# v after q and k, gelus of fc1 behind the next chunk's products, and two PSUM tiles let go one by one, in a two-layer kernel that a planner orders

## Chip, cores and metric

One core of a Trainium2 chip runs the whole kernel. Five engines work beside each other, each through its own queue in order: TensorE (PE, with PEld for its weight loads), VectorE (DVE), ScalarE (ACT), GpSimd (POOL) and SyncE (SP, which issues DMAs). The metric is the device time of one execution in microseconds (us); a kernel's time is the median of its runs.

## The reference

Two layers on x of shape (8, 192, 64, 64) in float32. Layer 0 is window attention that keeps 16 keys per query, and an MLP; layer 1 is a Fourier mixer with a tiny pointwise MLP on (real, imaginary), and an MLP. Cut to what matters:

```python
# layer 0, tokens of one image; windows of 8 x 8 tokens, 6 heads of 32
shortcut = layer_norm(xs)
q, k, v  = split(windows(shortcut) @ qkv_w.T + qkv_b)
attn = einsum(l2n(q), l2n(k)) * temperature
attn = where(attn >= 16th largest of the row, attn, -100) ; attn = softmax(attn + rpb)
x2  = shortcut + (attn @ v) @ proj_w.T + proj_b
x2  = x2 + gelu(layer_norm(x2) @ fc1_w.T + fc1_b) @ fc2_w.T + fc2_b
# layer 1
f   = fft2(layer_norm(x))                       # per channel, 64 x 64
h   = gelu([f.real, f.imag] @ fc1_w.T + fc1_b) @ fc2_w.T + fc2_b
x   = x + real(ifft2(h))
out = x + gelu(layer_norm(x) @ mlp1_w.T + mlp1_b) @ mlp2_w.T + mlp2_b
```

Gelu is the exact one; the Fourier transforms are matrix products.

## The kernel before

An image is cut into 8 bands of 512 tokens; the 192 channels are kept as 128 + 64, and the last 64 channels of two half bands are laid on 128 partitions, so that a product over 192 channels is one product on 128 rows of the array and two on 64 rows that run side by side. For each band of layer 0 there are `front` (transpose, normalization, products of q, k and v, norms of q and k), `attention` twice (half bands `hb`: scale q and k, transposes `qt`, scores `s`, top 16 on DVE, softmax, `at`, product with v `po`) and `back` (projection `pp`, then `mlp`). Layer 1 goes by groups of 16 channels: `forward` (products `fa` along rows of the transform and `fz` along the other axis), `pointwise` twice (products `fh`, gelu on ACT, products `fo`), `inverse` (`fb`, `fy`); and by bands: `leave` (`mlp`, transposes `pz`, store).

All these are Python generators. Each `yield op(engine, weight, mode, get, put, after, done)` offers one block of instructions to the planner `issue` (line 33), which keeps a clock for each engine in its own units, knows for each offered block when its inputs and its buffers are there, and always picks one of those that can begin first, with urgency by due time. The order in which blocks are picked is the order of instructions in each engine's queue. A generator offers its next block only when the last has been picked, so the order of `yield`s within a generator is a fixed order within that band's work, while different bands, layers and images are interleaved freely. `get` and `put` count buffers: `ps` are the PSUM tiles, of which there are four of two banks each, `h` the gelu outputs, `xa` scratch, and so on. `mode` names how the array is divided; the planner charges 20 units where it changes on PE and 130 units where ACT changes between exp and gelu. A block with `EITHER` goes to ACT or DVE, whichever the planner sees finish first; the scaling of q and k goes to POOL or DVE, the square to ACT or POOL.

The places that the change touches:

- `mlp` (from line 551): three chunks of fc1, `fp` = 0, 1, 2, each with a product on 128 rows (`part_a`, L587) and on 64 rows (`part_b`, L600); chunk 1 has them in the other order, so that the sequence of chunk 0, 1, 2 is 128, 64, 64, 128, 128, 64. After each chunk `gelu` (L571, two ACT instructions) is offered, which frees the chunk's PSUM tile. After all three, `mo` (L630) needs all three gelus.
- `front` (from line 643): for p = 0 and 1 (halves of the tokens) products of q and k into `pq` (L744 on 128 rows, L758 on 64, L761 the bias) and of v into `pv` (L745 and L758) are in the same blocks, and `pv` stays open over both. The first block asks for two PSUM tiles at once. `squares` copies `pq` out (L786), squares (L708 on ACT or L710 on POOL), sums (L712); after p = 1 `norms` raises to the power -1/2 on POOL for each half band (L730); `values` copies `pv` out.
- `forward` (from line 981): two PSUM tiles `fz` are copied into one SBUF tile (L1032) by two DVE instructions in one block, then a row is corrected (L1037).

Copies that can go to either engine are all recorded at L786.

Of the kernel before, what the change touches and what calls it, by code (L numbers as in the profile page):

```python
# [15 lines left out]
C = 192  # L16
# [3 lines left out]
BAND = 512  # L20
# [8 lines left out]
def op(engine, weight, mode=None, get="", put="", after=None, done=None, put_too=""):  # L29
    return engine, weight, mode, get.split(), (put + " " + put_too).split(), after, done  # L30
# [108 lines left out]
def kernel(  # L139
# [18 lines left out]
    nc = tc.nc  # L158
# [9 lines left out]
    def psum(name):  # L168
        return psp.tile([128, 2, 512], FP, tag="ps", name=name)
# [4 lines left out]
        ps=4, xt=XT_BUFS, xn=1, qk=1, vv=2, att=ATT_BUFS, qkt=1, sm=2, ot=1, hn=2, xa=2,  # L174
# [69 lines left out]
    wqkv = load_ab("wqkv", 3 * C)  # L244
# [29 lines left out]
    qb3 = ctile("qb3", [128, 2 * C], BF)  # L274
    ones3 = ctile("ones3", [128, 128], BF)
# [275 lines left out]
    def mlp(src, nm, w1, fc1_bias, w2, then=None):  # L551

        mv = yield from statistics(src, nm)
        yield op("pool", 0, get="xa")
        to, pair = tokens("xa", 2, f"xa_{nm}")
        last = yield from normalized(to, pair, src, mv, nm)
        if then is not None:
            yield then()
        yield op("pe", 66, "full", get="ps hn", put="xa", after=last)
        pc = flat(f"lc_{nm}")  # L560
        to_channels(pc, pair, to)
        done = yield op(EITHER, (80, 96), put="ps")
        hn = strip("hn", 2, f"hn_{nm}")
        copy(done, hn, pc[:, :ROW])
        hs = []

        def gelu(fp, ph):
            yield op("act", 138, "gelu", put="ps", done=("gelu", nm, fp))
            h = sb.tile([128, 2, BAND], FP, tag="h", name=f"h_{nm}_{fp}", bufs=H_BUFS)
            for k in range(2):  # L570
                nc.scalar.activation(  # L571
                    h[:, k].rearrange("p (t n) -> p t n", t=2),
                    ph[:, :, k * HALF : (k + 1) * HALF],
                    AF.Gelu,
                    bias=fc1_bias[:, 2 * fp + k : 2 * fp + k + 1],
                )
            hs.append(h)

        for fp in range(3):


            fs = [slice((2 * fp + k) * 128, (2 * fp + k + 1) * 128) for k in range(2)]

            def part_a(first):
                for k, f in enumerate(fs):
                    for t in range(2):
                        nc.tensor.matmul(  # L587
                            ph[:, t, k * HALF : (k + 1) * HALF],
                            w1[0][:, f],
                            hn[:, t * HALF : (t + 1) * HALF],  # L590
                            start=(first and k == 0),
                            stop=not first,
                            skip_group_check=True,
                        )

            def part_b(first):
                for k, f in enumerate(fs):
                    for t in range(2):
                        rows = slice(64 * t, 64 * t + 64)
                        nc.tensor.matmul(  # L600
                            ph[:, t, k * HALF : (k + 1) * HALF],
                            w1[1][rows, f],
                            hn[rows, BAND:ROW],
                            start=(first and k == 0),
                            stop=not first,
                            skip_group_check=True,
                        )
# [12 lines left out]
        last = [("gelu", nm, fp) for fp in range(3)]  # L620
        for half in range(2):
            if half == 0:
                yield op("pe", 384, "full", get="ps", after=last)
                acc = psum(f"mo_{nm}")
            else:
                last = yield op("pe", 384, "full", put="h h h")
            for f in range(3 * half, 3 * half + 3):
                for t, j in PAIRS:
                    q = 2 * t + j
                    nc.tensor.matmul(  # L630
                        acc[:, j, t * C : (t + 1) * C],
                        hs[f // 2][:, f % 2, q * 128 : (q + 1) * 128],
                        w2[:, f, ORDER[t]],
                        start=(f == 0 and t == 0),
                        stop=(f == 5),
                        skip_group_check=True,
                    )
        return acc, last
# [4 lines left out]
    def front(b, i):  # L643

        nm = f"{b}_{i}"
# [14 lines left out]
        done = yield op(EITHER, (80, 96), put="ps")  # L660
# [5 lines left out]
        last = yield from normalized(xt, pair, pair, mv, f"a{nm}")  # L666
# [7 lines left out]
        for t, j in PAIRS:  # L674
            q = 2 * t + j
            for h in range(2):
# [17 lines left out]
        places = ("qk", "h") if more else ("qk", "vv")  # L694
# [40 lines left out]
        def values(whole):  # L735
            done = yield op(EITHER, (80, 96), put="ps", after=[whole], done=("vv", b, i))
            copy(done, vv.rearrange("p t a c -> p t (a c)"), pv[:, :, : 2 * C])

        for p in range(2):
            def part_a(first):  # L740
                for t in range(2):
                    tok = xn[:, (2 * t + p) * 128 : (2 * t + p + 1) * 128]
                    flags = dict(start=first, stop=not first, skip_group_check=True)
                    nc.tensor.matmul(pq[:, t, : 2 * C], tok, wqkv[0][:, : 2 * C], **flags)  # L744
                    nc.tensor.matmul(  # L745
                        pv[:, t, p * C : (p + 1) * C], tok, wqkv[0][:, 2 * C :], **flags
                    )

            def part_b(first):
                flags = dict(skip_group_check=True, stop=not first)  # L750
                for to, cols in (
                    (pq[:, :, : 2 * C], slice(0, 2 * C)),
                    (pv[:, :, p * C : (p + 1) * C], slice(2 * C, 3 * C)),
                ):
                    for t in range(2):
                        rows = slice(64 * t, 64 * t + 64)
                        tok = xn[rows, BAND + p * 128 : BAND + (p + 1) * 128]
                        nc.tensor.matmul(to[:, t], tok, wqkv[1][rows, cols], start=first, **flags)  # L758
                for t in range(2):
                    rows = slice(64 * t, 64 * t + 64)  # L760
                    nc.tensor.matmul(  # L761
                        pq[:, t, : 2 * C], ones3[rows], qb3[rows], start=False, **flags
                    )
# [217 lines left out]
    def forward(b, n):  # L981

        nm = f"{b}_{n}"
# [12 lines left out]
        for q in range(4):  # L996
# [4 lines left out]
                start=True,  # L1001
                stop=True,
# [303 lines left out]
```

## Time and profile before

| what | value |
|---|---|
| median of 3 runs (lowest, highest) | 4932.9 us (4930.42, 4936.1) |
| the profiled execution's own time | 4943.11 us |
| its span, first to last instruction | 4941.3 us |
| mean granted TensorE clock | 0.977 |
| instructions in the span | 147,257 |
| largest groups on ACT: L1050 gelu of fh | 815.1 us busy, x768, mean 1112 ns |
| on POOL: L730 power of the norms | 551.9 us busy, x128, mean 4311 ns |
| on PE: L630 mo_b and mo_d | 518.0 and 512.3 us busy, x3072 each, mean 327 ns |
| ACT table loads before exp (L858), fh (L1050), h (L571) | x110, x64, x47, 1283 ns each |

In a line of a group, out<-in are the program's names, then come shapes, the count, busy time, the mean of one, and the engine's idle time before it with what ended most of it. A float32 matmul leaves two records. A wait's line has the engine and instruction that waited, after the arrow the one whose end released it, then the sum, the number of times and the longest, all in us. In a line of windows come the stretch, its length, then busy time and count of PE, PEld, DVE, ACT and POOL, the granted clock, the DMA share and GB/s.

### The profile page before, as it was taken

The numbers are of one execution on the slowest core, as the hardware profiler recorded it, in microseconds if no ns is written. First come the engines' busy times: TensorE is split into PE (matmuls) and PEld (weight loads), VectorE is DVE, ScalarE is ACT, GpSimd is POOL, SyncE is SP. The second block draws the span as 40 slices with busy tenths as digits, with TensorE's granted clock in tenths as the row PEclk, the third lists the DMA queues.
The fourth block names the chain that finished last, engine by engine and source line by source line (L and its number), as shares of the span: only waits on it lengthen the run. The fifth ranks groups of instructions, "written<-read, shape, count | busy, mean of one in ns | idle before, by whom it ended". The sixth has DMA issues, their size and how long they took to land.

```text
span 4941.3 us, 147257 instructions
## 1 busy us (share of the span) xinstructions
PE 4702.8 (95%) x63818; PEld 3780.0 (76%) x63818; DVE 2797.7 (57%) x10326; ACT 2744.7 (56%) x3866; POOL 2381.0 (48%) x2208
## 2 busy tenths in 40 slices
PE   6888999999999999999999999999999999999989
PEld 4667777886778877888678877788777887778768
DVE  6778566456665466655665556645666546562112
ACT  3555666446655566555755566645666456653553
POOL 5677555346554455454653555545555445541100
PEclk7898999999999999999999999999999999999999
DMA  2000000000000000000000000000000000000000
GB/s 55 11 8 11 9 9 5 23 14 9 9 12 17 18 6 9 13 19 15 9 5 14 22 14 6 9 14 24 9 6 9 20 18 9 2 2 20 9 2 26
DMA packets 54112, 64.09 MB, mean 13 GB/s; under 512 B 17583, under 2 KB 36218, under 8 KB 53466
## 3 DMA queue, kind: packets, MB, share of 16 engines
q1 hardware_dynamic: 53454, 54.68, 3.8%
q8 instruction: 502, 8.22, 0.7%
q14 instruction: 144, 1.18, 0.1%
q10 hardware_dynamic: 12, 0.00, 0.0%
HBM read 29.29 MB, written 25.17 MB: 11 GB/s over the span
## 4 chain that ended last, share of the span: by engine, by line
PE 85%; ACT 5%; DVE 5%; POOL 3%; issue 2%; DMA 0%; SPq 0%; ACTq 0%; DVEq 0%; POOLq 0%
PE mo_d L630 10%; PE mo_b L630 9%; PE fh L1067 8%; PE mh_d L587 7%; PE fo L1094 7%; PE mh_b L587 7%; PE mh_d L600 4%; PE mh_b L600 4%; PE pq L744 3%; ACT fh L1050 3%; PE qt L804 2%; PE fa L997 2%; PE at L871 2%; PE fb L1115 2%; PE fy L1142 2%
## 5 line engine op out<-in xcount | busy, mean ns | idle before, releaser
L1050 ACT ACTIVATE fh<-fh,ab 128x1024 f32<-128x1024 f32 x768 | 815.1, 1112 | 163.9 <-PE fh L1067 160.2
L854 POOL TENSOR_TENSOR s<-s,top 128x768 f32<-128x768 f32 x128 | 193.8, 1514 | 917.5 <-DVE s L851 870.8
L730 POOL TENSOR_TENSOR nrm<-nrm,mhalf 128x24 f32<-128x24 f32 x128 | 551.9, 4311 | 10.7
L630 PE MATMUL mo_b<-wfc,h_b 128*128 128x192 f32 x3072 | 518.0, 327 | 0.0
L630 PE MATMUL mo_d<-wmlp,h_d 128*128 128x192 f32 x3072 | 512.3, 327 | 0.0
L630 PEld LDWEIGHTS mo_b<-wfc,h_b 128*128 128x128 f32 x3072 | 499.2, 190 | 10.3 <-issue 5.8
L630 PEld LDWEIGHTS mo_d<-wmlp,h_d 128*128 128x128 f32 x3072 | 498.6, 190 | 7.2 <-issue 4.6
L1067 PE MATMUL fh<-fz,w1p 32*128 32x248 f32 (+1 forms) x6144 | 467.6, 404 | 30.1 <-ACT fh L1050 23.3
L571 ACT ACTIVATE h_d<-mh_d,fcb 128x512 f32<-128x512 f32 x384 | 242.1, 684 | 436.0 <-PE mh_d L600 278.1
L1067 PEld LDWEIGHTS fh<-fz,w1p 32*128 32x128 f32 x6144 | 293.0, 185 | 149.5 <-issue 67.3
L844 DVE MAX8 top<-s 128x8 f32<-128x64 f32 x1536 | 320.9, 209 | 129.0 <-ACT s L786 127.9
L1094 PE MATMUL fo<-fh,w2p 128*32 128x264 f32 (+1 forms) x6144 | 387.2, 389 | 3.9 <-ACT fh L1050 2.3
L846 DVE MAX8 top<-s 128x8 f32<-128x64 f32 x1536 | 349.9, 228 | 53.4
L587 PE MATMUL mh_b<-hn_b,wfc_a 128*128 128x256 f32 x1536 | 377.0, 389 | 3.2 <-ACT hn_b L786 1.9
L587 PE MATMUL mh_d<-hn_d,wmlp_a 128*128 128x256 f32 x1536 | 370.7, 386 | 0.8 <-ACT hn_d L786 0.8
L864 POOL TENSOR_TENSOR s<-s,rsum 128x768 f32<-128x768 f32 x128 | 191.2, 1494 | 300.4 <-DVE top L844 144.5
L587 PEld LDWEIGHTS mh_b<-hn_b,wfc_a 128*128 128x128 f32 x1536 | 280.0, 191 | 67.7 <-issue 26.5
L587 PEld LDWEIGHTS mh_d<-hn_d,wmlp_a 128*128 128x128 f32 x1536 | 280.6, 190 | 55.3 <-issue 18.1
L845 DVE MATCH_REPLACE8 s<-top,s 128x64 f32<-128x64 f32 x1536 | 320.3, 209 | 0.1
L1094 PEld LDWEIGHTS fo<-fh,w2p 128*32 128x32 f32 x6144 | 185.6, 111 | 152.8 <-issue 33.4
L571 ACT ACTIVATE h_b<-mh_b,fcb 128x512 f32<-128x512 f32 x384 | 243.1, 686 | 97.3 <-PE mh_b L600 50.6
L1180 DVE TENSOR_TENSOR zt<-mo_d,xy 128x768 f32<-128x768 f32 x64 | 61.3, 957 | 377.2 <-PE mo_d L630 345.5
(220 smaller groups left out, 9311.2 us busy)
## 6 DMA issues: line engine op xcount, KB each, us to landing
xin<-in_x SPq DMA_DIRECT2D x64, 256.0 KB
out<-z SPq DMA_DIRECT2D x64, 256.0 KB
xin<-in_x SPq DMA_DIRECT2D x128, 64.0 KB
out<-z SPq DMA_DIRECT2D x128, 64.0 KB
wfc<-in_wfc SPq DMA_DIRECT2D x1, 576.0 KB
wmlp<-in_wmlp SPq DMA_DIRECT2D x1, 576.0 KB
wfc_a<-in_wfc SPq DMA_DIRECT2D x1, 384.0 KB
wfc_b<-in_wfc SPq DMA_DIRECT2D x2, 192.0 KB
```

Of the source, the lines that this page charges most:

```text
L571: nc.scalar.activation(h[:, k].rearrange("p (t n) -> p t n", t=2), ph[:, :, k * HALF : (k + 1) * HALF], AF.Gelu, bias=fc1_bias[:, 2 * fp + ...
L587: nc.tensor.matmul(ph[:, t, k * HALF : (k + 1) * HALF], w1[0][:, f], hn[:, t * HALF : (t + 1) * HALF], start=(first and k == 0), stop=not ...
L600: nc.tensor.matmul(ph[:, t, k * HALF : (k + 1) * HALF], w1[1][rows, f], hn[rows, BAND:ROW], start=(first and k == 0), stop=not first, skip ...
L630: nc.tensor.matmul(acc[:, j, t * C : (t + 1) * C], hs[f // 2][:, f % 2, q * 128 : (q + 1) * 128], w2[:, f, ORDER[t]], start=(f == 0 and t ...
L730: nc.gpsimd.tensor_tensor(nf, nf, mhalf[:, :24], ALU.pow)
L844: nc.vector.max(first, of)
L845: nc.vector.match_replace(s2, first, of, -3.0e38)
L846: nc.vector.max(top[:, k // 4, k % 4, 8:16], s2)
L854: nc.gpsimd.tensor_tensor(s, s, top[:, :, :, 0:1].to_broadcast(shape), ALU.subtract)
L1050: nc.scalar.activation(hs[hf, k], ph, AF.Gelu, bias=ab[:, 0:1])
L1067: nc.tensor.matmul(phs[k // 2][:, k % 2, cols], w1p[i][rows, hf].rearrange("p h v -> p (h v)"), fz[rows, :] if rhs is None else zu[rows, : ...
L1094: nc.tensor.matmul(po[rows, :] if i == 0 else pou[rows, :, 1 : U - 1], w2p[i][:, hf].rearrange("p a v -> p (a v)"), hs[hf, k // 2][:, k % ...
```

## The change

Three edits, and with them the order that the planner makes of everything.

1. In `front` the products of q and k for p = 0 and p = 1 come first, in blocks of their own (`qk_a`, `qk_b`), each with its `squares` offered behind it; the products of v for both p follow in two blocks, 128 rows and then 64 rows, into a `pv` that is asked for only then. The first block asks for one PSUM tile in place of two.
2. In `mlp` the gelu of chunk `fp - 1` is offered after the products of chunk `fp`; the last gelu follows after the loop. Since a gelu no longer follows directly on its products, it names them in `after`.
3. In `forward` the two copies out of `fz` are two blocks, each of which lets one PSUM tile go; the correction of the row goes with the second.

Matmuls, copies, and their sizes are the same; the number of ACT table loads and the engine of a copy, scale or square follow from the planner.

```diff
-        def gelu(fp, ph):
-            yield op("act", 138, "gelu", put="ps", done=("gelu", nm, fp))
+        def gelu(fp, ph, last):
+            yield op("act", 138, "gelu", put="ps", after=[last], done=("gelu", nm, fp))
...
-                yield op(
+                last = yield op(
                     "pe", weight, kind, get=get, put="hn" if fp == 2 and n == 1 else "", after=after
                 )
...
-            yield from gelu(fp, ph)
+            if fp > 0:
+                yield from gelu(fp - 1, *held_)
+            held_ = ph, last
+        yield from gelu(2, *held_)
         last = [("gelu", nm, fp) for fp in range(3)]
...
+        def qk_a(pq, p, first):
+            for t in range(2):
+                tok = xn[:, (2 * t + p) * 128 : (2 * t + p + 1) * 128]
+                nc.tensor.matmul(
+                    pq[:, t, : 2 * C],
+                    tok,
+                    wqkv[0][:, : 2 * C],
...
+        def qk_b(pq, p, first):
...
+        yield op("pe", 128, "full", get=f"ps {places[0]} {places[1]}", after=[normal, "qkv"])
+        pq = psum(f"pq_{nm}_0")
+        qk_a(pq, 0, True)
+        last = yield op("pe", 80, "row64")
+        qk_b(pq, 0, False)
+        yield squares(0, pq)
+        yield op("pe", 80, "row64", get="ps", after=[])
+        pq = psum(f"pq_{nm}_1")
+        qk_b(pq, 1, True)
+        yield op("pe", 128, "full")
+        qk_a(pq, 1, False)
+        yield squares(1, pq)
+        yield op("pe", 128, "full", get="ps", after=[])
+        pv = psum(f"pv_{nm}")
         for p in range(2):
-            def part_a(first):
...
-            if p == 0:
-                yield op("pe", 192, "full", get=f"ps ps {places[0]} {places[1]}", after=[normal, "qkv"])
-                pq, pv = psum(f"pq_{nm}_{p}"), psum(f"pv_{nm}")
-                part_a(True)
-                yield op("pe", 112, "row64")
-                part_b(False)
-            else:
-                yield op("pe", 112, "row64", get="ps", after=[])
-                pq = psum(f"pq_{nm}_{p}")
-                part_b(True)
-                whole = yield op("pe", 192, "full", put="xn")
-                part_a(False)
-            yield squares(p, pq)
+            for t in range(2):
+                nc.tensor.matmul(
+                    pv[:, t, p * C : (p + 1) * C],
+                    xn[:, (2 * t + p) * 128 : (2 * t + p + 1) * 128],
+                    wqkv[0][:, 2 * C :],
...
+        whole = yield op("pe", 64, "row64", put="xn")
+        for p in range(2):
...
         yield values(whole)
...
-        yield op("dve", 118, put="ps ps", done=("fz", b, n))
         fz = sb.tile([128, 16 * U], FP, tag="fz", name=f"fz_{nm}", bufs=2)
         for k in range(2):
+            yield op("dve", 43 + 33 * k, put="ps", done=("fz", b, n) if k else None)
             nc.vector.tensor_copy(
```

More of the change, by code (lines that the diff above doesn't have):

```diff
@@ L737, in values @@
             copy(done, vv.rearrange("p t a c -> p t (a c)"), pv[:, :, : 2 * C])
-        for p in range(2):
-            def part_a(first):
[L741 to L763, printed above, removed]
-            if p == 0:
-                yield op("pe", 192, "full", get=f"ps ps {places[0]} {places[1]}", after=[normal, "qkv"])
-                pq, pv = psum(f"pq_{nm}_{p}"), psum(f"pv_{nm}")
-                part_a(True)
-                yield op("pe", 112, "row64")
-                part_b(False)
-            else:
-                yield op("pe", 112, "row64", get="ps", after=[])
-                pq = psum(f"pq_{nm}_{p}")
-                part_b(True)
-                whole = yield op("pe", 192, "full", put="xn")
-                part_a(False)
-            yield squares(p, pq)
@@ new lines, in qk_a @@
+        def qk_a(pq, p, first):
[5 more added lines that the diff above has]
+                    wqkv[0][:, : 2 * C],
+                    start=first,
+                    stop=not first,
+                    skip_group_check=True,
+                )
+        def qk_b(pq, p, first):
+            flags = dict(skip_group_check=True, stop=not first)
+            for t in range(2):
+                rows = slice(64 * t, 64 * t + 64)
+                tok = xn[rows, BAND + p * 128 : BAND + (p + 1) * 128]
+                nc.tensor.matmul(
+                    pq[:, t, : 2 * C], tok, wqkv[1][rows, : 2 * C], start=first, **flags
+                )
+            for t in range(2):
+                rows = slice(64 * t, 64 * t + 64)
+                nc.tensor.matmul(pq[:, t, : 2 * C], ones3[rows], qb3[rows], start=False, **flags)
@@ new lines, in front @@
+        pv = psum(f"pv_{nm}")
+        for p in range(2):
+            for t in range(2):
+                nc.tensor.matmul(
+                    pv[:, t, p * C : (p + 1) * C],
+                    xn[:, (2 * t + p) * 128 : (2 * t + p + 1) * 128],
+                    wqkv[0][:, 2 * C :],
+                    start=(p == 0),
+                    stop=False,
+                    skip_group_check=True,
+                )
+        whole = yield op("pe", 64, "row64", put="xn")
+        for p in range(2):
+            for t in range(2):
+                rows = slice(64 * t, 64 * t + 64)
+                nc.tensor.matmul(
+                    pv[:, t, p * C : (p + 1) * C],
+                    xn[rows, BAND + p * 128 : BAND + (p + 1) * 128],
+                    wqkv[1][rows, 2 * C :],
+                    start=False,
+                    stop=True,
+                    skip_group_check=True,
+                )
```

## The prediction

> **What bounds the kernel now.** I read the engine totals and the 40 slices first, then the windows, PE's waits in the opening and in the long middle, and last single stretches of the timeline. Engine totals and the chain's shares from the page:
>
> ```profile
> PE 4702.8 (95%) x63818; PEld 3780.0 (76%) x63818; DVE 2797.7 (57%) x10326; ACT 2744.7 (56%) x3866; POOL 2381.0 (48%) x2208
> ...
> PE   6888999999999999999999999999999999999989
> PEclk7898999999999999999999999999999999999999
> ...
> PE 85%; ACT 5%; DVE 5%; POOL 3%; issue 2%; DMA 0%; SPq 0%; ACTq 0%; DVEq 0%; POOLq 0%
> ```
>
> PE is busy for 95% of the span and is 85% of the chain; no other engine passes 57%. Only the first four slices (500 us) leave PE clearly idle, and there the granted clock is below full as well. Three windows size this (first number after the stretch is PE's busy time):
>
> ```profile
> 0.00:625.00 625.00, 524.17 (x6540) 420.97 (x6540) 452.70 (x1774) 317.02 (x488) 409.64 (x356) 0.89 0.07 19
> 625.00:4700.00 4075.00, 3958.34 (x54711) 3181.09 (x54710) 2303.91 (x8432) 2323.90 (x3230) 1951.67 (x1816) 0.99 0.04 12
> 4700.00:4941.30 241.30, 220.26 (x2572) 177.99 (x2568) 41.14 (x121) 103.81 (x149) 19.68 (x36) 0.98 0.05 14
> ```
>
> PE idles 100.8 us in the opening, 116.7 in the middle, 21.0 at the end: 238.5 together. The change can save only there, or in how tightly the busy part runs. What PE waits for, opening first, then middle (total us, times, longest):
>
> ```profile
> PE qt L804 <- DVE qk L798: 27.4, 4, 12.1
> PE qt L804 <- POOL qk L798: 21.2, 3, 14.0
> PE s L821 <- ACT qkt L786: 14.2, 12, 2.4
> PE at L871 <- POOL s L864: 12.0, 7, 5.3
> ```
>
> ```profile
> PE fh L1067 <- ACT fh L1050: 23.3, 26, 1.6
> PE fz L1022 <- ACT fh L1050: 15.3, 16, 1.9
> PE lc L539 <- ACT fh L1050: 10.2, 16, 1.0
> ...
> PE lt L653 <- ACT fh L1050: 9.0, 6, 1.5
> PE qt L804 <- ACT fh L1050: 8.1, 19, 0.5
> ```
>
> Half of the opening's idle time, 48.6 us in seven waits, is qt (the transposes that begin attention of a band) waiting for scaled q and k, which is the end of `front`'s chain: product, copy, square, sum, norms on POOL, scale. In the middle the names differ but the releaser is one: ACT's gelu of fh. lt and lc do not read fh, so what they wait for is the PSUM tile that this gelu empties; these five lines are 65.9 of 116.7 us.
>
> The busy part hides a second loss. Timeline of PE near the end (start, us, instruction):
>
> ```profile
> 4854.10 1.13 PE L600 MATMUL mh_d<-hn_d,wmlp_b 64*128 64x256 f32 x8
> 4855.16 8.07 PE L630 MATMUL mo_d<-wmlp,h_d 128*128 128x192 f32 x48
> ...
> 4866.82 2.00 PE L600 MATMUL mh_d<-hn_d,wmlp_b 64*128 64x256 f32 x16
> 4868.74 1.99 PE L587 MATMUL mh_d<-hn_d,wmlp_a 128*128 128x256 f32 x8
> ```
>
> From start to start, eight L600 records (products on 64 rows) take 1.06 us where a product on 128 rows follows, and a run of sixteen takes 1.92, so the first eight, which their own kind follows, take 0.86. A change of tile size costs some 0.1 to 0.2 us. Over all 1,242 gap-free changes between 625 and 4700 us, the same subtraction (start to start, less the median of the same group followed by its own kind) gives a mean of 0.107 us.
>
> [...] the opening has waits of 12 and 14 us and a mean clock of 0.89, against 0.99 in the middle. [...] all 222 loads in this trace have a mean of 1283 ns.
>
> **The change part by part.** No matmul is added or removed (33,832 in both builds, two records each less what the trace lost). All order comes from the planner, so I compared the order of the two builds on every engine.
>
> (1) v behind q and k. Of the old order, five of the six v parts of a band stand on PE before q and k's last product. A v part (L745 or L758) takes 0.32 to 0.33 us from start to start at full clock: 2 x 0.33 + 0.32 + 0.32 + 0.33 = 1.63 us. At the clock of the first band (starts at 18.07, 20.00, 21.56, 24.08, 25.46 us) the same five take 0.64 + 0.77 + 0.33 + 0.33 + 0.33 = 2.40. The chain to qt starts that much earlier and the v products fill time in which PE idled. Where the chain ends a wait, that is the seven waits: 7 x 1.63 = 11.4 us. The v copy comes later; its reader (po) stands after qt, s, top-16 and at, whose DVE part alone is 12 x 0.74 us, so it is covered. If that cover went, po would wait 0.8 us (ACT copy of vv). A PSUM tile of v is also held for less: the PE work that stands between its first and last product falls from 10.3 to 4.7 us, and for a q,k tile from 4.6 to 3.5 (columns in the two orders, by 3.92 us for the 12 x 192 of half an mo, narrower tiles in proportion).
>
> (2) What the planner makes of that on POOL. The longest wait (14.04 us, at 338.8) has POOL in it: sq 1.47, norms twice 4.7, then s of another band 1.49 and 1.80, then the scale 2.19. In the new order of this band (7 of the first image) the two s steps stand ahead of the norms, where POOL idled 7.55 us, the square is ACT's (0.84) and the scale DVE's (0.96 to 1.16), and the pf products (L294, 3.3 us on PE between two q,k parts) stand before the band. After the 1.63 already counted: 1.49 + 1.80 + 2.19 - 1.1 = 4.4, square 0.6, pf 3.3: 8.3 us. Over the kernel 41 scales go from POOL to DVE and 10 squares to ACT: POOL -41 x 1.57 - 10 x 1.5 = -79 us; ACT gains about 78 us, mostly by copies of vv (40 x 0.80) and xn (38 x 0.48) and normalizations (72 x 0.54), less 14 table loads (18 us) and 28 copies of ot (9); DVE loses about 46. None of these is the bound.
>
> So (1) and (2) are worth at most 11.4 + 8.3 = 19.7 us, if each wait shrinks fully and nothing else is late, and about nothing at least, if DVE (72% busy in the opening, 81% between 250 and 500 us) or POOL's s steps are late next. The lower end could only pass below nothing through a worse order, which is rival C. I take 12: seven tenths of the shifts (8.0) and half of the POOL part (4.1).
>
> (3) gelus offered later. Products of chunk 0 and 1 now stand together: "0, 64 rows" directly before "1, 64 rows" in 101 of 128 mlps (9 before), and "1, 128 rows" before "2, 128 rows" in 76 (1 before). Other work takes some of it back: v's own 64-row part is one change more, and fh, fo and fb now stand between other things. Tile size changes from one matmul to the next: 2,215 before, 2,146 after. 69 x 0.107 = 7.4 us, all of it on PE. The price: a tile of mh waits longer for its gelu, and the last two gelus (2 x 2 x 0.69 us) stand behind chunk 2 instead of one; mo starts up to 1.4 us later, and products of another band or of layer 1 cover it. Queued behind the late gelus on ACT are the fh gelus which free PSUM.
>
> (4) fz's tiles freed singly: one copy (0.42 us) earlier in the plan, 96 times. [...] nothing.
>
> PSUM waits in the middle: the order shows both signs. Tenancies of a PSUM slot that follow within 1 us of PE work (same reckoning) on the former's last product: 214 before, 247 after; within 2 us: 927 and 891. Bounds: a quarter of the 65.9 us less (-16), a half more (+35, a late gelu in front of a third of the fh gelus). I take 0.
>
> Sum: -7.4 - 12 = -19.4 us. The profiled execution took 4943.1 us (span 4941.3), 10.2 above the median of the runs, 4932.9; the difference is applied to the median: 4913.5.
>
> **Rivals.** A, as summed: 4913.5, own range 4898 to 4925. For it: the waits have one chain in common. B: [...] the opening's waits end with POOL's norms and DVE's top-16 as before: 4932.9 - 7.4 = 4925.5. For it: DVE's 81%. Against: POOL and ACT idle for 7.6 and 4.8 us ahead of that chain at 311 to 321 us. C, slower: a held mh tile plus delayed gelus make the four PSUM tiles late for layer 1 in the middle; 35 us of PE idle more than I take, 4913.5 + 35 = 4948.5 (4960 if the opening gives nothing). For it: 33 more tenancies within 1 us, each a wait of up to about 1 us as in the lines shown; from 19.4 us of growth in these waits the kernel is slower. Against: mh's own tiles are re-let less tightly (within 2 us 41 before, 14 after). D: the full 19.7 in the opening and a quarter of the PSUM waits gone: 4932.9 - 7.4 - 19.7 - 16.5 = 4889. That the change does nothing is excluded by the orders.
>
> **How the numbers follow.** A 0.48, B 0.12, C 0.24, D 0.16. A measurement of this kernel tells 0.2% (9.9 us) from no change, so faster is under 4923.0, slower over 4942.8. Faster: A 0.46, D 0.16, B 0.04 = 0.66. Within: A 0.02, B 0.08, C 0.02 = 0.12. Slower: C 0.22. The range reaches from below D to near C: 4880 to 4955; A's own stands above.
>
> **What would show it.** PE busy falls by about 7 us at equal record count; the qt waits in the first 625 us fall from 48.6 to under 38, the 14 us one to about 5; ACT table loads 208; POOL about 2302, ACT about 2823 us; the waits on ACT fh in the middle within 15 us of 70. It is wrong if idle time in the middle grows by over 15 us, if qt's waits stay, or if the opening's idle time reappears at another line.

## The result, and the profile after

The changed kernel takes 4954.12 us (median of 7 runs, 4948.38 to 4963.0); the kernel before took 4936.1 beside it. The ratio is 1.0034, interval [1.0022, 1.0046]: slower by a third of a percent, against a forecast of 4913.5. The profiled execution took 4963.0 us with a span of 4961.2, which is 19.9 above the span of before (both profiled executions are slower than their medians, by 9 and 7 us). Slow executions are left out of all medians and ratios; there was one, of 18,943.93 us, of before_order_v_moved below.

The engine totals, PE's slices and the chain's shares of the page after:

```profile
PE 4695.1 (95%) x63818; PEld 3773.3 (76%) x63818; DVE 2810.0 (57%) x10238; ACT 2804.3 (57%) x3991; POOL 2331.6 (47%) x2157
...
PE 74%; POOL 11%; DVE 6%; ACT 5%; issue 3%; SPq 0%; DMA 0%; ACTq 0%; POOLq 0%; DVEq 0%
```

PE is busy for 7.7 us less, which is the size that the step on tile sizes had; whether it is that step is taken up below. POOL, 3% of the chain before, is now 11%. The three windows, with PE's busy time first:

```profile
0.00:625.00 625.00, 514.93 (x6378) 408.47 (x6379) 444.78 (x1720) 320.97 (x495) 397.50 (x346) 0.89 0.08 19
625.00:4700.00 4075.00, 3940.43 (x54418) 3173.56 (x54416) 2324.46 (x8395) 2363.28 (x3331) 1911.55 (x1773) 0.99 0.04 12
4700.00:4961.20 261.20, 239.70 (x3032) 191.30 (x3024) 40.72 (x124) 120.09 (x166) 22.51 (x39) 0.97 0.05 14
```

PE idles 110.1, 134.6 and 21.5 us: 9.3 more in the opening, 17.9 more in the middle, 0.5 at the end. So 27.6 us more idle less 7.7 us less busy make the 19.9. What PE waits for, opening first, then middle:

```profile
PE at L895 <- POOL s L888: 45.0, 7, 11.8
PE qt L828 <- ACT s L882: 12.1, 1, 12.1
PE s L845 <- issue: 10.8, 2, 10.4
...
PE qt L828 <- DVE qk L822: 6.8, 2, 3.6
```

```profile
PE at L895 <- POOL s L888: 24.8, 25, 2.0
PE fz L1046 <- ACT fh L1074: 10.8, 13, 2.1
...
PE qt L828 <- ACT fh L1074: 3.0, 6, 0.7
PE fh L1091 <- ACT fh L1074: 2.8, 10, 0.3
```

The qt waits of the opening did fall, from 48.6 us to 18.9 in the lines shown, and the fh waits of the middle from 23.3 to 2.8. A line that was small before has grown: `at`, the transposes of the softmax, waiting for the division by the row sum (L888), which is POOL's last step. It had 12.0 us in the opening and 1.6 in the middle. One of its long waits, PE's row and then POOL's rows ahead of it (start, us, instruction):

```profile
188.06 1.54 PE L895 MATMUL at<-ident,s 128*128 128x128 f32 x6 [11.13 <-POOL s L888]
```

```profile
177.27 4.19 POOL L733 TENSOR_TENSOR nrm<-nrm,mhalf 128x24 f32<-128x24 f32 x1
...
182.08 4.20 POOL L733 TENSOR_TENSOR nrm<-nrm,mhalf 128x24 f32<-128x24 f32 x1
...
186.53 1.47 POOL L888 TENSOR_TENSOR s<-s,rsum 128x768 f32<-128x768 f32 x1
```

DVE had the row sum's reciprocal ready at 179.06, yet the division runs at 186.53: both norms of another band, some 9.6 us with their small steps, stand ahead of it in POOL's queue. The planner has set the norms first. On POOL a division stands directly behind a norm at 25 places (11 before), of which only 3 are ahead of layer 1 (2 before). v_alone below, with edit 1 alone, has 9 such places in all; so that q and k are ready sooner is not shown to be the reason.

The wait without a releaser ("issue", 10.4 us) is of another kind. PE stops inside one group of `s`:

```profile
85.02 0.70 PE L845 MATMUL s<-qkt 32*64 32x64 f32 x38
96.15 0.50 PE L845 MATMUL s<-qkt 32*64 32x64 f32 x10 [10.44 <-issue]
```

Before had this gap too, of 6.25 us; I took no note of it. The DMA view of after for 93.5 to 94.2 us (queue: packets, MB, share) holds one large packet among many of 4 bytes:

```profile
q1 hardware_dynamic: 244, 0.00, 17.9%
q8 instruction: 1, 0.02, 9.3%
```

Queue 8, which the profile labels "instruction", moves 502 packets of 16 KB in the whole execution, one for every 254 of PE's 127,636 records. That they carry PE's own instructions is my inference, from this count and from where PE's gaps end. Of the gaps over 0.5 us without a releaser, all 16 of before (25.4 us together) and 22 of the 24 of after (34.4 us) end 2.0 to 3.05 us after such a packet began, while windows of this length behind all 502 packets cover 11% of the span. So in this pair of executions 9.0 of the 27.6 us stand behind such packets, and the 10.4 us gap ends 2.4 us after the packet of 93.8 us.

The length of this gap changes from one execution to the next, with the same order on every engine. fz_alone, one of the experiments below, has the order of before on PE, DVE, ACT and POOL through the whole opening; its row at this place is

```profile
87.90 0.57 PE L821 MATMUL s<-qkt 32*64 32x64 f32 x31 [1.72 <-issue]
```

Six kernels have before's order from the start to past this place (before, fz_alone, before_order_gelus_moved, gelu_alone, gelu_and_fz, before_table131), with gaps of 1.7 to 7.5 us. Six have after's (after, after_table131, after_penalty19, after_penalty21, after_order_norm_moved, v_alone), with gaps of 6.4 to 10.4.

### The profile page after: what moved, and what is told of

Its sections match the earlier page's. It is cut to its first block, busy times and chain, and to the rows that moved or that the text cites. A ratio compares the mean times of both kernels' runs of the same rounds, so it can differ in the third digit from the quotient of the medians.

```text
span 4961.2 us, 147132 instructions
## 1 busy us (share of the span) xinstructions
PE 4695.1 (95%) x63818; PEld 3773.3 (76%) x63818; DVE 2810.0 (57%) x10238; ACT 2804.3 (57%) x3991; POOL 2331.6 (47%) x2157
## 4 chain that ended last, share of the span: by engine, by line
PE 74%; POOL 11%; DVE 6%; ACT 5%; issue 3%; SPq 0%; DMA 0%; ACTq 0%; POOLq 0%; DVEq 0%
PE mo_b L633 10%; PE mo_d L633 9%; PE fh L1091 6%; PE mh_d L587 6%; PE fo L1118 6%; PE mh_b L587 5%; POOL nrm L733 4%; PE mh_d L600 3%; PE pq L745 3%; PE mh_b L600 3%; ACT fh L1074 2%; PE qt L828 2%; PE fy L1166 2%; PE fa L1021 2%; PE fb L1139 2%
## 5 line engine op out<-in xcount | busy, mean ns | idle before, releaser
L633 PEld LDWEIGHTS mo_b<-wfc,h_b 128*128 128x128 f32 x3072 | 501.5, 191 | 11.7 <-issue 4.8
L1091 PE MATMUL fh<-fz,w1p 32*128 32x248 f32 (+1 forms) x6144 | 454.4, 401 | 6.2 <-ACT fh L1074 2.8
L888 POOL TENSOR_TENSOR s<-s,rsum 128x768 f32<-128x768 f32 x128 | 193.2, 1513 | 193.0 <-DVE rsum L886 141.6
L822 DVE TENSOR_TENSOR qk<-qk,nrm 128x768 f32<-128x768 f32 x102 | 169.3, 1667 | 175.0 <-POOL nrm L734 175.0
```

The source lines that it names most:

```text
L633: nc.tensor.matmul(acc[:, j, t * C : (t + 1) * C], hs[f // 2][:, f % 2, q * 128 : (q + 1) * 128], w2[:, f, ORDER[t]], start=(f == 0 and t ...
L1091: nc.tensor.matmul(phs[k // 2][:, k % 2, cols], w1p[i][rows, hf].rearrange("p h v -> p (h v)"), fz[rows, :] if rhs is None else zu[rows, : ...
```

## The experiments

Each was compared with the kernel before on its own chip, so ratios are the thing to compare. "First fa" is the start of layer 1's first product; PE is busy for 371 to 387 us ahead of it in the orders drawn by the planner. It is read from the one traced execution of each kernel.

### One edit alone, and the planner's charge

The edits apart, each planned anew; and the kernel before with one unit more for a change of tile size.

```diff
 v_alone:          edit 1 of the change, mlp and forward as before
 gelu_alone:       edit 2, front and forward as before
 fz_alone:         edit 3, front and mlp as before
 before_penalty21, on the kernel before:
-    change = {"pe": 20, "act": 130, "dve": 0, "pool": 0}
+    change = {"pe": 21, "act": 130, "dve": 0, "pool": 0}
```

> Products of v behind q and k alone; gelus and fz as before. Theory V (the norms come to POOL earlier and stand ahead of the softmax's last step there, so that the transposes at wait in place of qt): slower than before by 0.2% or more, at waits on POOL s over 40 us in all, qt waits in the first 625 us under 30. Theory G (the later gelus make the four PSUM tiles late): faster by 5 to 15 us, since this part only shortens the opening. Theory N (any new order of the planner scatters by this much): anywhere within 20 us of before, and the idle time lies at other lines than in the full change. Tile size changes 2,228, 13 more than before[...].

> Gelus offered one chunk later alone. Theory V: faster by 5 to 12 us, 79 fewer tile size changes (2,136) at 0.107 us. Theory G: slower by 10 us or more, waits on ACT fh in the middle over 90 us (66 to 70 before). Theory N: anywhere within 20 us of before.

> The two PSUM tiles of fz let go singly, alone. Theories V and G: within 5 us of before, 30 fewer tile size changes (2,185), 3 us. Theory N: anywhere within 20 us of before[...].

> The kernel before with one unit in the planner changed, the charge for a change of mode on PE 21 in place of 20: no part of the change, but a wholly new order (53 fewer tile size changes). It measures what reordering alone does. Theories V and G: within 8 us of before, faster if anything[...]. Theory N: off by 10 us or more, either way.

| run | median us | ratio, interval |
|---|---|---|
| v_alone | 4955.21 | 1.0032 [1.0020, 1.0045] |
| gelu_alone | 5016.88 | 1.0158 [1.0143, 1.0173] |
| fz_alone | 4938.57 | 1.0002 [0.9993, 1.0010] |
| before_penalty21 | 4994.50 | 1.0110 [1.0095, 1.0125] |

The three parts add to 1.9% and the whole is 0.34%: the edits don't add. And the last line changes no product and no size, only a price in the planner, and costs three times what the change costs. An order drawn anew can by itself be worth tens of microseconds (57 here), so no part can be priced by planning it once. This holds for v_alone too, though it is as slow as the whole change and has the `at` waits that theory V had forecast for it: 41.3 us in all, 13.6 before.

### The order held fixed

I wrote out the order of blocks that the planner had picked and played it back, so that one thing at a time could be moved:

```diff
-    while live:
-        best, ready = {}, {}
...
+    for step in PLAN:
+        name, engine = step.split(":")
+        task = next(t for t in live if t["id"] == name)
+        advance(task, (engine, 0))
```

In before's order, before_order_v_moved puts the two blocks of v behind q and k's last block in every band; before_order_v_opening does it in the first ten bands (`if NB * b + i < 10`). In after's order, after_order_norm_moved puts the second norm behind the division at the 25 places where it stood directly ahead of it on POOL.

> The kernel before with its order of all blocks written out in place of the planner, and only one thing moved in it: a band's v products stand directly behind its last q,k product. So edit 1 without a new plan. Theory P (the edit does what the prediction said, and the plan that the planner makes of it is what costs): qt waits in the first 625 us fall from 48.6 to 37 to 41, the first fa starts 6 to 11 us earlier than at 471.5; over the whole, 81 more tile size changes (2,296) cost 8.7 us, so 4930 to 4940. Theory V (norms that come earlier make at wait, in any order): no gain in the opening, first fa not before 469 us, at waits on POOL s over 25 us, total 4943 or more.

> The order before, written out, with v moved behind q and k only in the first ten bands, where qt waits. Theory P: first fa 6 to 10 us earlier than before's 471.5 as in the run with v moved everywhere, [...] (17 more tile size changes, 1.8 us, in place of 81): 5 to 9 us under before. If the middle gives the opening's gain back: within 3 us of before.

> The changed kernel with its order written out, and only this moved: in the 25 places where the softmax's last POOL step (division) stands directly behind the second of two norms, that norm goes behind it. Theory V: the at waits behind norms shrink by up to 4.9 us each, the waits of 11.1 and 11.7 us in the opening to 6 to 7, all at waits on POOL s from 70 to 50 or less; total 4936 to 4946, that is 8 to 18 us under the change. If qt or DVE's scale is as late anyway (the wait only moves back): within 5 us of the change, 4950 to 4959.

| run | median us | ratio, interval | first fa (before 471.5, after 484.2) |
|---|---|---|---|
| before_order_v_moved | 4937.79 | 1.0003 [0.9991, 1.0015] | 463.7 |
| before_order_v_opening | 4928.14 | 0.9982 [0.9974, 0.9990] | 462.2 |
| after_order_norm_moved | 4954.82 | 1.0036 [1.0022, 1.0049] | 479.6 |

With the order fixed, first fa comes 8 to 9 us earlier than in before's trace. Over the whole kernel nothing of it is left in before_order_v_moved, where PE is 13.4 us longer busy (81 tile-size changes more, 8.7 us by the price of 0.107; the rest has no account). Moved in ten bands alone, it stays a gain, of 0.18% over 22 executions. Part of this comes with the clock: the mean granted clock of these 22 is 0.9795, of the 30 of before beside them 0.9778, and at the same clock (0.978 to 0.981) the kernel with v moved is 1 to 4 us faster.

It isn't the gain that I had worked out, though. The opening's waits in before_order_v_opening (0 to 480 us):

```profile
PE qt L823 <- DVE qk L817: 27.2, 4, 10.8
PE qt L823 <- POOL qk L817: 25.2, 2, 13.7
PE s L840 <- ACT qkt L805: 12.7, 10, 2.4
PE at L890 <- POOL s L883: 7.5, 9, 2.6
```

The qt waits are not smaller (52.4 us; 48.6 before). Against the same groups in before's trace the lead is 1.7 us at the third qt (69.1 us), 4.3 at the fifth (102.4) and 9.6 at the sixth (107.9); from there to first fa it keeps within 7.5 and 11.1. All is won in the first three bands, and more than half of it between the fifth and the sixth. There PE of before waits 5.3 us for `at`, and this wait descends from the gap at 94.6 us: the projection pp stands behind the gap on PE, the addition of pp on DVE waits for it (timeline of before, DVE),

```profile
99.81 0.96 DVE L945 TENSOR_TENSOR xt<-pp,xt 128x768 f32<-128x768 f32 x1 [9.64 <-PE pp L935]
```

and the row sum that `at` needs stands behind the addition. In before_order_v_opening the instruction packet moves at 76.9 us, not 92.2, the gap is absent, and the same addition waits 1.4 us.

Before's trace is the latest of its order at the sixth qt. Over fz_alone, with the same order and the gap of 1.7 us, the lead at first fa (465.5) is 1.8 us for before_order_v_moved and 3.3 for before_order_v_opening. Five traces have v moved in before's opening (these two, both_moved, table131_v_opening and v_alone_opening_replaced, all described below), and none has the gap. Against the six named above with before's order, their mean lead is 1.2 us at the third qt, 2.7 at the fifth and 7.4 at the sixth. By this comparison edit 1 itself is worth some 1 to 3 us there; the rest is that this order misses the gap.

In after_order_norm_moved the two long `at` waits shrank (11.1 to 6.3 us, 11.7 to 6.2), qt's grew by 4.2 and 4.4, and the ratio stayed (1.0036; 1.0034), where theory V had forecast 8 to 18 us less; the intervals leave room for a few us. The block of norms is late for one reader or for the other; moving it between them mostly moves the wait.

### Late gelus, and both edits, in before's order

Of 128 mlps, 81 can have their gelus late in before's order without a fifth PSUM tile; before_order_gelus_moved does that, both_moved adds v in ten bands. v_alone_opening_replaced has v_alone's order with the opening of before_order_v_moved in front.

> Edit 2 without a new plan: the order of the kernel before, written out, in which for 81 of the 128 mlps chunk 1's products are drawn up behind chunk 0's (in 59 of them chunk 2's first too) and the gelus follow a chunk later; the other 47 stay, since a fifth PSUM tile would be open. Tile size changes 2,132, 83 fewer than before. Theory P (the edits do what the prediction said, the new plan costs): [...] 4926 to 4934 where before is 4937. Theory G (tiles held longer, gelus late): idle time in the middle grows by more [...], 4942 or more, waits on ACT fh and at lines of mh and mo up by over 9 us.

> The last two together: v moved in the first ten bands and the gelus of 81 mlps moved, all else in the order before. Theory P: the two gains add, 12 to 17 us under before (0.25 to 0.35%), under both kernels. Theory G: no better than before.

> Edit 1's own plan (the run with v alone, 4955), but all blocks up to the first fa in the order before with v moved, and the rest in the plan's order. If the loss of edit 1's plan lies in its opening (first fa at 481.6 against 463.7): 4935 to 4942. If it lies in the middle: 4949 or more, with first fa near 464 all the same.

They took 5048.93 (1.0226 [1.0206, 1.0247]), 5039.51 (1.0209 [1.0191, 1.0226]) and 4953.50 us (1.0029 [1.0014, 1.0045]). PE's waits over the whole of before_order_gelus_moved:

```profile
PE fa L962 <- POOL xf L956: 21.2, 8, 3.3
...
PE mo_d L595 <- ACT h_d L529: 16.1, 11, 2.6
```

Before, mo_d waited for nothing (0.0 us). I had written that other products cover its later start; in an order that isn't drawn again, mo stands at the head of PE's queue, waits, and holds up everything behind it. The idle time of the middle is 183.8 us, against 116.7, and PE is busy at half clock for 207 us, against 166. That the wait of mo brings the others on was not traced: gelu_alone, drawn anew, has hardly any wait at mo (1.0 us), yet fa waits 27.4 us for POOL there too, and it is 1.6% slower.

In the third run PE has before_order_v_moved's order up to the place of first fa, but then products of mlp come first, so its first fa can't be compared. Its opening idles 6.3 us less than v_alone's and the time is the same within the intervals: that v_alone's loss lies in its opening (4935 to 4942 forecast) is not borne out.

### The planner drawn again

Four charges, both kernels; gelu_and_fz has edits 2 and 3.

```diff
 after_penalty21:   "pe": 20 -> 21 in the changed kernel
 before_penalty19, after_penalty19:   "pe": 20 -> 19
 before_table131, after_table131:     "act": 130 -> 131
```

> The changed kernel with the planner's charge for a change of mode at 21 in place of 20: all three edits, another order. Theory N (the order drawn decides, by tens of us): at least 10 us away from the change's 4954, either way. Theories V and G (the edits cost what they cost): 4946 to 4962.

> The kernel before with the same charge at 19: no edit, another order. Theory N, with the order before as an unusually good one: 4950 to 5000, with idle time of PE in the middle of 130 to 170 us in place of 117. If 21 was unusually bad instead: within 10 us of 4937.

> The changed kernel, charge for a change of mode 19. Theory N (which order is drawn decides, the three edits as such are worth little): anywhere from 4935 to 4995, like the orders of the kernel before (4937, 4972, 4994). If the edits cost by themselves under any order: 4950 to 4975, close to the two orders of the changed kernel seen (4954, 4971).

> The kernel before, charge for a table change 131: an order that differs from before's in about a quarter as many lines of PE as charge 21 does. Theory N: 4940 to 4975, slower than before in proportion. If the order before is of the usual kind and 19 and 21 were unusual: within 8 us of 4937.

> The changed kernel, charge for a change between exp and gelu on ACT 131 in place of 130: a third new order of the changed code. As for charge 19: N 4935 to 4995 with a spread of 20 or more over the four; fixed cost of the edits 4950 to 4975.

> Edits 2 and 3 without edit 1, planner's order: a second order of the late gelus with v as before. If late gelus cost by themselves when v holds its PSUM tile long (as the run with gelus alone, 5017, and the fixed order, 5049, say): 4985 or more. Theory N: 4940 to 4995, and gelus alone was a bad order.

| charge | before's code | changed code | at <- POOL, opening | gap near 95 us |
|---|---|---|---|---|
| 20, 130 | 1 | 1.0034 [1.0022, 1.0046] | 12.0 -> 45.0 | 6.2 -> 10.4 |
| 20, 131 | 0.9983 [0.9972, 0.9995] | 1.0016 [1.0006, 1.0025] | 23.8 -> 43.2 | 4.5 -> 7.3 |
| 21, 130 | 1.0110 [1.0095, 1.0125] | 1.0074 [1.0058, 1.0091] | 19.9 -> 41.4 | 3.4 -> 9.5 |
| 19, 130 | 1.0075 [1.0058, 1.0092] | 1.0181 [1.0165, 1.0197] | 7.3 -> 47.9 | 6.5 -> 10.0 |

gelu_and_fz took 4985.88 us, 1.0094 [1.0077, 1.0111].

The changed code is slower at three charges and faster at one. The differences in ratio are +0.34, +0.33, -0.36 and +1.06%. PE idles in the middle between 114 and 164 us in all these orders, and is busy at half clock for 132 to 215 us over the whole. At charge 19 it is 135 us in before's code and 215 in the changed code; by an estimate from the time of the same products at half and at full clock in these traces, this makes some 30 of the 59 us between the two spans. Two things hold in every pair of traces: in the opening the `at` waits take over from qt (whose sum falls from 40 to 57 us to 20 to 30), and the gap near 95 us is longer. PE's idle time ahead of first fa is 94 to 101 us in the four traces of before's code and 102 to 108 in those of the changed code. But these are not four draws of the opening: the changed code has one order on all engines up to 139 us at all four charges, and before's code has one up to 211 us at 130 and 131. That this one order is slower is measured; that the edits make slower orders in general is not.

At charge 19 the changed code shows my slower rival as I had described it, fh, lc and fa late behind the gelu of fh:

```profile
PE fh L1091 <- ACT fh L1074: 25.7, 36, 2.3
PE lc L539 <- ACT fh L1074: 20.6, 13, 3.2
...
PE fa L1021 <- ACT fh L1074: 19.0, 15, 2.4
```

### Two last runs: another fixed order, and the gap's cause

table131_v_opening plays back the order of before_table131 with v moved in the first ten bands.

> The order of before_table131 written out (no planner), with v's products behind q and k in the first ten bands only, as in before_order_v_opening. Theory P (the first edit is worth its opening wait in any order held fixed, about 5 to 9 us there): 4921 to 4926 us, 5 to 9 under the 4930.6 of before_table131; first fa some 8 us earlier than its 472.4. Rival (what the opening gains is given back later in the order, as in v_alone_opening_replaced): within 3 us of 4930, with the middle's idle time 6 us or more above its 112.5.

It took 4923.45 us, 0.9972 [0.9962, 0.9982] of before, and 7 us under before_table131's median; first fa stands at 463.3 (472.4). It has the lowest ratio here, but its interval overlaps those of before_table131 and before_order_v_opening, so a gain over these is not shown. Nor is its opening quite another order: on PE it is that of before_order_v_opening up to 294 us. Its lead has the same shape as in the other fixed order: 3.7 us at the third qt, 9.1 at the sixth, 9.1 at the last, and the gap near 95 us (4.5) is gone.

The other run takes the 4-byte packets out of after's order. In the stretch of the gap SP issues the loads of n1g, a table of norm factors for layer 1. The DMA view of after, 82 to 94 us, and SP's row:

```profile
DMA packets 2510, 0.03 MB, mean 3 GB/s; under 512 B 2508, under 2 KB 2508, under 8 KB 2508
```

```profile
81.58 14.88 SPq L450 DMA_DIRECT2D n1g<-in_n  x4
```

Each of eight loads takes every fourth element of a row: 768 packets of 4 bytes for 3.0 KB. Of the 2510 packets in these 12 us, 2508 are under 512 B.

```diff
-            for k in range(4):
-                src = bass.AP(
-                    n1t.tensor, n1t.offset + c * 2 * HC + k, [[0, 32], [4, 24], [1, 1]]
-                )
-                dst = n1g[32 * k : 32 * k + 32, 24 * c : 24 * c + 24]
-                nc.sync.dma_start(dst.unsqueeze(2), src)
+            src = bass.AP(n1t.tensor, n1t.offset + c * 2 * HC, [[0, 128], [1, HC]])
+            nc.sync.dma_start(n1w[:, c, :], src)
...
+        for k in range(4):
+            nc.vector.tensor_copy(
+                n1g[32 * k : 32 * k + 32].rearrange("p (c j) -> p c j", c=2),
+                n1w[32 * k : 32 * k + 32].rearrange("p c (j k) -> p k c j", k=4)[:, k],
+            )
```

> The order of the changed kernel written out, and one thing altered: n1g is no longer loaded by eight DMAs of 4-byte pieces (8 x 768 packets) but as whole rows of 384 bytes by two DMAs, and spread by four small copies on DVE in the block that follows. In all runs so far with a PE gap of the kind 'issue' between 84 and 97 us, the gap ends 2.2 to 2.4 us after an instruction packet of 16 KB has moved. Theory F (the fetch of PE's instructions stands behind the 4-byte packets): the gap of 10.4 us at 85.7 to 96.2 falls under 1 us, the first fa comes 8 to 11 us before 484.2, and the time is 4943 to 4947 us. Rival (the gap is PE's own, or its time is found again at the next wait on POOL): first fa within 3 us of 484, time within 4 us of 4954.

It took 4946.16 us (21 runs), 1.0020 [1.0012, 1.0027]: 8 us under the changed kernel, 7 by the ratios, whose intervals just overlap (1.0034 [1.0022, 1.0046]). PE's timeline around the place of the gap, and SP's of the loads:

```profile
84.49 0.80 PE L804 MATMUL s<-qkt 32*64 32x64 f32 x48
85.22 0.66 PE L498 MATMUL lc<-ident,xt 128*128 128x128 f32 x4
```

```profile
74.07 0.43 SPq L404 DMA_DIRECT2D n1w<-in_n  x1
...
74.88 0.34 SPq L404 DMA_DIRECT2D n1w<-in_n  x1
```

All 48 products of `s` run without a stop, the instruction packet that moved at 93.8 us moves at 81.1, first fa comes at 473.2 (11.0 earlier), and PE's gaps behind instruction packets fall from 34.4 to 23.8 us. In six traces of after's order the gap was 6.4 us or more, so that this one has none is hardly chance: in this order the gap came with the 4-byte packets (82 to 96 us now has 306 packets, 16 of them under 512 B). That it was a fetch of PE's instructions, late behind them, is inferred from the packet that moves earlier; the trace shows no fetch as such. The waits of the opening are now:

```profile
PE at L854 <- POOL s L847: 33.1, 6, 11.7
PE qt L787 <- ACT s L841: 12.2, 1, 12.2
PE qt L787 <- POOL qk L781: 11.7, 1, 11.7
```

With the gap went one of the long `at` waits (11.8 us at 116.6 in after, 8.2 to 11.8 in the six traces with the gap), and 11.7 us of qt stand in its place. So of the 33 us by which `at` grew, some 12 came from the gap and not from the norms. PE is 7.5 us less busy than in after, though its products and their order are the same: it ran 140 us at half clock, 154 in after. The fix is independent of the change: before has the same gap, and this load was not tried there or in the two faster orders.

## Why the prediction was wrong

The forecast was 19.4 us less and the change took 18 us more. What failed are the terms of the opening, taken as -12 us and measured as 9.3 us more idle time, and of the middle, taken as 0 and measured as 17.9 more. Two of the prediction's own signs of being wrong came true: the middle's idle time grew by over 15 us, and the opening's came back at another line.

- **Tile sizes (-7.4).** The size came out, the reason is not shown. PE's busy time fell by 7.7 us, but the granted clock in the traces is 1.0 or 0.5, and at half clock the same products take nearly twice as long (in before's trace a qt takes 214 ns from start to start, 113 at full clock). PE was busy at half clock for 166 us before and 154 after; reckoned product by product, from start to start at either clock, this makes some 4 to 6 of the 7.7 us. That both numbers agree is at least in part luck.
- **Planner's shifts.** Right in sign for two engines: 208 table loads, as said; POOL 2331.6 (2302 forecast), ACT 2804.3 (2823). DVE was to lose about 46 us and gained 12.3: its scales take 1.667 us on average, where step (2) used 0.96 to 1.16.
- **Step (1), 7 x 1.63 us.** The qt waits fell below the 38 us that I had named, to 18.9, but "if each wait shrinks fully and nothing else is late" is where it failed: the `at` waits of the opening rose from 12.0 to 45.0 us. Two of them, 22.8 us together, waited for the softmax division behind the norms in POOL's queue; a third, 11.8, followed from the gap near 95 us. In an order held fixed the qt waits don't fall at all. The mean lead there is 2.7 us over the first three waited-for bands, where the step gives 4.9, and 4.7 more in what that gap had delayed. In before_order_v_opening, set against before, there is nothing at the four later waits. Why those four gain nothing is open.
- **Step (2), 8.3 us at the wait of 14.04.** The s steps came ahead of the norms at one place, and the norms ahead of the division at others; only the first was in the sum. That qt no longer waits in the changed kernel, but the `at` just ahead of it waits 11.7 us. Rival B named POOL's norms as what could end the waits, as qt's releaser; they did, as that of `at`, and the cost went below nothing, which I had left to rival C alone.
- **The cost not in the sum.** The wait list of before had "s <- issue" with 6.2 us in one wait, and I gave it no cause. It rose to 10.4, and 9.0 of the 27.6 us of added idle time stand behind instruction packets in the two profiled executions.
- **Step (3), the late gelus at no cost.** "Products of another band or of layer 1 cover it" failed when tried: +2.3% in before's order, with mo waiting 16 us. In the changed kernel's own order this wait doesn't show.
- **Step (4), fz's tiles, taken as nothing.** This was my estimate. No run has the edit in a fixed order; fz_alone, drawn anew, took 1.0002 [0.9993, 1.0010] of before.
- **Middle taken as 0.** It grew by 17.9. Rival C foretold the sign and not the place: the waits on ACT's fh fell from 70 to 53 us, those without a releaser rose from 19 to 28, and `at` behind POOL's division from 1.6 to 24.8. The last is not shown to be the loss: fz_alone has 27.0 us of it in the middle, idles there for 119.2 us, and is as fast as before. What made the middle longer stays open. The time, 4954.1, fell inside the range by 1 us.

What the runs don't settle is the split of the 18 us among the edits. The orders drawn at four charges differ by more than that in either code.

## What to carry to other kernels

Where a greedy planner sets all order, price an edit twice: in the old order held fixed, which shows what it does itself, and in several drawn orders, which show how large the draw is; one drawn order shows neither. Kernels that share their order over a stretch are repeats of that stretch: look at how far these differ before reading a lead from two traces. A gain at one reader of an engine's queue can be a cost at the next one, as here, where qt's waits of the opening fell from 48.6 to 18.9 us and those of `at` rose from 12.0 to 45.0: look at what stands behind the long block that moves forward. And a wait of the saturated engine without a releaser can have a cause too: set its end beside the instruction packets; 38 of the 40 such gaps over 0.5 us, in the traces of before and after, end 2.0 to 3.05 us after the start of one.

## What the runs showed of the hardware

PE stood still for 10.4 us in after without a releaser, until 2.4 us after a 16 KB instruction packet had begun to move; 2.2 to 2.5 us pass from the start of such a packet to PE's next product in all 14 runs that had a gap between 84 and 97 us, of 1.7 to 10.4 us. In after_order_whole_rows, without the 4-byte packets, the packet moves at 81.1 us in place of 93.8 and there is no gap.

The executions of one kernel differ with their mean granted clock. The 30 executions of before beside before_order_v_opening take 4953 us on average at 0.975, 4938 at 0.978 and 4925 at 0.981. So PE's busy time in two traces can differ with nothing changed on PE, as by 7.5 us between after and after_order_whole_rows (154 and 140 us at half clock).

The scaling of q and k on DVE, with two SBUF operands in float32, takes longer when it stands beside POOL's work. Its group in the page after:

```profile
L822 DVE TENSOR_TENSOR qk<-qk,nrm 128x768 f32<-128x768 f32 x102 | 169.3, 1667 | 175.0 <-POOL nrm L734 175.0
```

Alone, or while POOL does the 24-column power, the mean is 0.95 us in both traces (72 cases); where a step of POOL of 128x768 overlaps it, it was 1.66 before (18 cases) and 1.95 after (73). With 41 scales moved from POOL to DVE, those on DVE are the 102 of this line, at 1.667 us each.
